# A LoRA-plus-paged-attention kernel: first adapters loaded by a register's number, row numbers on GpSimd, gathers, weight reads and the last outputs in other places

## The chip, the cores and the metric

One core of a Trainium2 chip runs the whole kernel. The metric is the device time of one execution in microseconds; the time before is the median of three runs.

## The reference, cut to what matters

All tensors are float32. There are B = 8 sequences of S = 128 rows and HID = 512 columns, 16 adapters of 512 x 512, 32 query heads and 8 key heads of D = 128, and a cache of 64 pages of 32 positions, of which every sequence uses 16 pages (L = 512 positions).

```python
x = x + einsum("bsi,boi->bso", x, weight[adapter_ids])       # one adapter for each sequence
q, k, v = x @ Wq.T, x @ Wk.T, x @ Wv.T                       # 32, 8 and 8 heads of 128
q, k = rope(rmsnorm(q) * q_norm_w, pos), rope(rmsnorm(k) * k_norm_w, pos)   # pos = seqlen + row
k_all = concat(k_cache[block_table], k)                      # 512 cached positions, then 128 new ones
v_all = concat(v_cache[block_table], v)
scores = q @ k_all.T * SCALE, with cached positions >= seqlen masked
o = softmax(scores) @ v_all                                  # each key head serves 4 query heads
out = x + o @ Wo.T
```

## The kernel before, in words

**Tiling.** The eight key heads are cut into G = 4 groups of two (GK = 2), with the eight query heads that belong to them (GQ = 8). A step is one group of one sequence; there are 32 steps, group by group, eight sequences in each (L216). A step has eight score slots, h = 0 to 7, one for each query head: j = h // 4 is the key head. In a slot (L942 to L1045) TensorE multiplies q by all 640 keys into PSUM (`sc`, L953), VectorE (DVE) adds the mask and takes the minimum of the row (L963; q is scaled negatively, so that is the maximum), ScalarE (ACT) takes the exponential with its sum (L979), VectorE the reciprocal (L1021), and GpSimd (POOL) scales the row (`p`, L1028). One slot later VectorE transposes the 32 x 32 blocks of `p` into `tp` (L808). After four slots `tp` is sent to DRAM (`xp`, L826) and read back with whole blocks exchanged (`pT`, L835), so that the transposition costs TensorE nothing. q (`tq`, `xq`, `qT`) and the cached keys (`tk`, `xk`, `kT`) go the same way; all these DMAs stand in SP's queue, in program order.

**The rest of a step.** Between the scores TensorE gets pieces of a list `main` (L917 to L940), dealt out by cost over the eight slots (L1008 to L1015): for the step that follows, the projections `kv`, `q0` and `q1` (`project`, L649, four matmuls of 128 x 512 each); for the step before, the values `o` of its two key heads (`values`, L770, five matmuls each), and its output `out` (`output`, L786, eight matmuls). From step 6 on ("early") the projections of kv and q0 come ahead of the first values. In group 0 the adapter's product `y` of a later sequence (`lora_y`, L526), its transposed weights `lw` (`turn_lora`) and the transposes of x (`turn_x` before the product is added, `turn_x1` after) come on top; their slots are written out by hand in L224 to L245. What a finished group of matmuls still needs on the other engines is put into a list `pending` and run in the next slot.

**Normalization.** `rotate` (L585) squares q on ScalarE, multiplies by the rotary tables CW and SW on VectorE and adds on GpSimd (L617, L624). `norm_scales` (L626) makes the scale on GpSimd (`ss`, `rs`, L631, L632); ScalarE then applies it (L637). Every engine works in the order in which its instructions were issued, so a scale waits behind whatever stands ahead of it on GpSimd.

**Gathers.** GpSimd issues the indirect DMAs: `kc` (L563) and `vc` (L569), four for each step and each kind, one for 128 cached positions, and the adapters' weights (`gather_lora`, L202). kc has one buffer, vc has two. Their row numbers `key_ix` and `val_ix` are computed at the start (L303). In step i the kc of step i + 2 is issued after slots 2 and 3 (in step 0 after 4 and 5), and the vc of step i + 1 after slots 5 and 6 (L1031 to L1038).

**Weights of later groups.** A piece of weights (128 x 512) is loaded by ScalarE's queue (`load_next`, L270), transposed in 32 x 32 blocks by VectorE and sent to DRAM (`send_weights`, L460), and read back with the blocks exchanged (`receive_weights`, L471), all on ScalarE's queue. The slots of these turns and reads, counted as 8 x step + h, are in L255 to L267; kv, q0 and q1 of the next group are read back in the group's last but one and last step, Wo's pieces in the second step of the new group. Each of the tiles kv, q0, q1, o0 and o1 has one buffer.

**Start and end.** The order of the start is written out in L862 to L911: small tables, the angles of the rotary embedding (`rope_angles`, L366), row numbers, then for sequence 0 the transposed x, kv weights, adapter (`lw`), the product `y`, q0 weights, x again with the product added, and the first projections. Transposes go through PSUM tiles of the pool `ps_mm`, which has four. ScalarE copies most of them out. In the last step the second half of p is transposed by TensorE (`pt`, L818), and behind the loop stand the last values and the last output (L1048 to L1056).

Of the kernel before, what the change touches and what calls it, by code (L numbers as in the profile page):

```python
# [18 lines left out]
P = 128  # L19
# [33 lines left out]
def lora_then_paged_attention(  # L53
# [47 lines left out]
    nc.sync.dma_start(out=ids_i, in_=adapter_ids.partition_broadcast(P))  # L101
# [43 lines left out]

    load_first("kv", 0, 2, nc.sync)
    load_first("kv", 2, 2, nc.scalar)
    bt_i = work.tile([P, 4, S], I32, tag="oT0", name="bt_i")
# [6 lines left out]
    nc.scalar.dma_start(out=wn[:, 0, :], in_=q_norm_w.partition_broadcast(P))  # L155
    nc.scalar.dma_start(out=wn[:, 1, :], in_=k_norm_w.partition_broadcast(P))
# [28 lines left out]
    for m in masks:  # L185
        nc.gpsimd.memset(m[:, :, LC, :], 0.0)


    lora_ix = const.tile([P, B], I32, name="lora_ix")
    nc.vector.scalar_tensor_tensor(  # L190
        out=lora_ix,
        in0=ids_i,
        scalar=float(HID // 4),
        in1=par.to_broadcast([P, B]),
        op0=ALU.mult,
        op1=ALU.add,
    )
    lora_rows = lora_w.rearrange("m (p j) i -> (m p) (j i)", j=4)

    lraw = {}  # L200

    def gather_lora(b, dst=None):  # L202
        if dst is None:
            dst = lora.tile([P, 4, REP, QK], FP, tag="raw", name=f"lraw_{b}")
            dst = dst.rearrange("p a r k -> p (a r k)")[:, 0 : 4 * HID]
        lraw[b] = dst
        nc.gpsimd.indirect_dma_start(
            out=dst,
            out_offset=None,
            in_=lora_rows,  # L210
            in_offset=bass.IndirectOffsetOnAxis(ap=lora_ix[:, b : b + 1], axis=0),
        )
# [11 lines left out]
    for i, (g, b) in enumerate(steps):  # L224
        if i == 0:
            at(i, 1, True, lambda: turn_x1(1))
            at(i, 3, False, lambda: turn_q(0, 1))
            at(i, 7, False, lambda: turn_q(1, 0))
            for n, h in enumerate((5, 6, 6, 7)):
                at(i, h, False, lambda n=n: turn_weights(("o0", 0, n)))  # L230
            for n, h in enumerate((7, 8, 9, 10)):
                at(i, h, False, lambda n=n: turn_weights(("o1", 0, n)))
        if i == last:
            at(i - 1, 6, False, lambda: turn_q(last, 0))
            at(i, 2, True, lambda: turn_q(last, 1))
        at(i, 2, True, lambda i=i: turn_k(i, 1), 1)
        if i < last:
            at(i, 6 if i else 7, False, lambda i=i: turn_k(i + 1, 0), 1)
        if g == 0 and b + 2 < B:
            at(i, 0, True, lambda b=b: turn_x(b + 2))  # L240
            for c in range(KC):
                at(i, c if i else c + 2, False, lambda b=b, c=c: turn_lora(b + 2, c))
            at(i, 8, True, lambda b=b: turn_x1(b + 2))
# [11 lines left out]
    for g in range(1, G):  # L255
        before = 8 * B * (g - 1)
        for k, kind in enumerate(("kv", "q0", "q1")):
            for n in range(4):
                turn_when[before + 9 + 3 * (4 * k + n)] = len(turns_of)
                turns_of.append((kind, g, n))  # L260
                h = (2, 3, 5)[k]
                read_at(before + 8 * (B - 2) + h + n, (kind, g, n))
        for k, kind in enumerate(("o0", "o1")):
            for n in range(4):
                turn_when[before + 46 + 3 * (4 * k + n)] = len(turns_of)
                turns_of.append((kind, g, n))
                read_at(8 * (B * g + 1) + k + n, (kind, g, n))  # L267
# [9 lines left out]


    gather_lora(0, first["lora"])
    load_first("q0", 0, 4, nc.gpsimd)  # L280
    gather_lora(1)

    def more_loads():

        nc.vector.memset(first["q1"][:, 0:1], 0.0)
        load_first("q1", 0, 4, nc.sync)
        load_x(1)
        load_x(2)

        for k in range(2):  # L290
            for n in range(4):
                t = (acc, x1T)[k][B - 4 + n]
                raw[f"o{k}", 0, n] = t if k == 0 else t.rearrange("p c s -> p (c s)")
                nc.sync.dma_start(out=raw[f"o{k}", 0, n], in_=weight_rows(f"o{k}", 0, n))


# [6 lines left out]
    def row_numbers():  # L303
        sel = const.tile([P, 3], FP, name="sel")
        for k in range(3):
            nc.vector.tensor_scalar(sel[:, k : k + 1], inner, 8.0 * (k + 1), None, ALU.is_ge)

        sk = const.tile([P, 1], FP, name="sk")
        nc.vector.scalar_tensor_tensor(
            out=sk, in0=inner, scalar=4.0, in1=quad, op0=ALU.mult, op1=ALU.add  # L310
        )
        for k in range(3):
            nc.vector.scalar_tensor_tensor(
                out=sk, in0=sel[:, k : k + 1], scalar=-32.0, in1=sk, op0=ALU.mult, op1=ALU.add
            )
        nc.vector.tensor_scalar(sk, sk, float(G), None, ALU.mult)
        sv = const.tile([P, 1], FP, name="sv")
        nc.vector.tensor_scalar(sv, inner, float(G), None, ALU.mult)
        temp = work.tile([P, GK, D], FP, tag="k", name="pages").rearrange("p h d -> p (h d)")
        bt_f = temp[:, 0 : 4 * B * LC].rearrange("p (c q) -> p c q", q=4)  # L320
        page = temp[:, 4 * B * LC : 5 * B * LC]
        step = temp[:, 5 * B * LC : 6 * B * LC]
        nc.vector.tensor_copy(bt_f, bt_i)
        nc.vector.tensor_copy(page, bt_f[:, :, 0])
        for k in range(3):
            nc.vector.tensor_tensor(step, bt_f[:, :, k + 1], bt_f[:, :, k], ALU.subtract)
            nc.vector.scalar_tensor_tensor(
                out=page, in0=step, scalar=sel[:, k : k + 1], in1=page, op0=ALU.mult, op1=ALU.add
            )
        nc.vector.scalar_tensor_tensor(  # L330
            out=key_ix[:, 0, :],
            in0=page,
            scalar=float(PSIZE * G),
            in1=sk.to_broadcast([P, B * LC]),
            op0=ALU.mult,
            op1=ALU.add,
        )
        for r in range(4):
            rows = slice(32 * r, 32 * r + 32)
            nc.vector.scalar_tensor_tensor(  # L340
                out=val_ix[rows, 0, :],
                in0=bt_f[rows, :, r],
                scalar=float(PSIZE * G),
                in1=sv[rows, :].to_broadcast([32, B * LC]),
                op0=ALU.mult,
                op1=ALU.add,
            )
        for g in range(1, G):
            nc.vector.tensor_scalar(key_ix[:, g, :], key_ix[:, 0, :], float(g), None, ALU.add)
            nc.vector.tensor_scalar(val_ix[:, g, :], val_ix[:, 0, :], float(g), None, ALU.add)  # L350
# [148 lines left out]
    def group(name, pieces, after):  # L499
# [3 lines left out]
        def piece(k, operands):  # L503
            if k == 0:
                if len(pending) > 1:
                    run(pending)
                y[0] = ps_mm.tile([P, HID], FP, tag="mm", name=name)
# [7 lines left out]
    def add_to_acc(b, store=False):  # L515
        def after(y):
            def add():
                nc.vector.tensor_tensor(acc[b], y, acc[b], ALU.add)
                if store:
                    nc.sync.dma_start(out=out[b], in_=acc[b])  # L520
# [249 lines left out]
    def values(i, j):  # L770
# [8 lines left out]
        def after(o):  # L779
            s.oT[j] = work.tile([P, REP, S], FP, tag=f"oT{j}", name=f"oT_{i}_{j}")  # L780

            pending.append(lambda: nc.scalar.copy(s.oT[j].rearrange("p h s -> p (h s)"), o))  # L782
# [3 lines left out]
    def output(i):  # L786
        g, b = steps[i]
        s = st[i]
        return group(
            f"out_{i}",  # L790
            [
                lambda h=h: (s.oT[h // 4][:, h % 4, :], weights_of(f"o{h // 4}", h % 4))
                for h in range(GQ)
            ],
            add_to_acc(b, g == G - 1),
# [66 lines left out]
    on_act, on_vec = nc.scalar.copy, nc.vector.tensor_copy  # L862
    table_set(AF.Sin)
    rope_angles()
    more_loads()
    row_numbers()
    turn_x(0, on_act)
    for n in range(4):
        turn_weights(("kv", 0, n), on_act)
    rope_cos()  # L870
    rope_table(1)
# [4 lines left out]
    for c in range(KC):  # L876
        turn_lora(0, c, on_act)
    for _, f in lora_y(0):
        f()
    for n in range(4):  # L880
        turn_weights(("q0", 0, n), on_act)
    flush()
    turn_x1(0, on_vec)
    rope_table(0)
# [13 lines left out]
    run(pending)  # L898
    for c in range(LC):
# [9 lines left out]
    make_mask(0)  # L909

# [4 lines left out]
    for i, (g, b) in enumerate(steps):  # L915
# [19 lines left out]
        if early:  # L935
# [3 lines left out]
        if i and i != last - 1:  # L939
            main += output(i - 1)  # L940
        unit = None
        for h in range(8):  # L942
# [88 lines left out]
            if i < last:  # L1031
                k = h - 2 if i else h - 4
                if k in (0, 1) and i + 1 < last:
                    gather_k(i + 2, 2 * k)
                    gather_k(i + 2, 2 * k + 1)
                if h in (5, 6):
                    gather_v(i + 1, 2 * h - 10)
                    gather_v(i + 1, 2 * h - 9)  # L1038
# [10 lines left out]
    pieces = output(last)  # L1049
    for part in (values(last, 0), pieces[0:4], values(last, 1), pieces[4:]):  # L1050
# [52 lines left out]
```

## Time and profile before

| what | value |
|---|---|
| median of 3 runs | 1225.86 us (1223.85 to 1227.68) |
| the profiled execution's own time | 1230.35 us |
| its span | 1228.5 us |
| mean granted clock of TensorE | 0.987 |
| DMA traffic | 328.26 MB, 267 GB/s in the mean |
| scores, L953 | 1024 matmuls (two forms), 321.6 us |
| values, L509 `o` | 640 matmuls, 305.5 us |
| projections of q, L509 `pj_q` | 512 matmuls, 238.7 us |
| output, L509 `out` | 512 matmuls, 235.1 us |
| projections of kv, L509 `pj_kv` | 256 matmuls, 118.1 us |
| GpSimd: gathers of kc and vc | 256, about 1.0 us each |
| GpSimd: scaling of p | 252, 0.80 us each |

The page gives busy times of each engine in one execution. PE is TensorE's matmuls, PEld its weight loads, which run beside them; a float32 matmul appears as two instructions. "Idle before" is the time in which an engine stood still ahead of an instruction, and the releaser is what ended it. The waits list adds up these idle times for each pair of waiting and releasing instruction. The chain lists, in order of time, the work that led to the last instruction. SPq and ACTq are the DMA issues of SP and ScalarE.

### The profile page before, as it was taken

To read this page: it belongs to the slowest core of one execution; us is meant where nothing else is said; L and a number is where in the kernel's file an instruction comes from. 1 tells how busy PE (TensorE), PEld (TensorE's weight loads), DVE (VectorE), ACT (ScalarE), POOL (GpSimd) and SP (SyncE) were. 2 spreads that over 40 slices of the span, in tenths; PEclk is the share of its full clock that TensorE was granted. 3 is DMA by queue.
4 is the path that set the end of the run, shared out by engine and by line. 5 is a ranking of instruction groups with operands and counts; after the bars stand their busy time and mean duration, and the time that the engine had idled before them with its cause. 6 is when DMAs were issued, how large, how long until landed. Compare 5 with 4: busy or idle time off the path is not lost.

```text
span 1228.5 us, 12918 instructions
## 1 busy us (share of the span) xinstructions
PE 1190.2 (97%) x3392; PEld 578.0 (47%) x3392; DVE 733.7 (60%) x1681; ACT 529.8 (43%) x1649; POOL 672.1 (55%) x765
## 2 busy tenths in 40 slices
PE   6979999999899999999999999999999999999988
PEld 4535544554444444444444444444444444444433
DVE  5455566656666666666666666666666655566631
ACT  4445444444444444444444444444444444444432
POOL 5463555454655655566556555666556555666340
PEclk8989999999999999999999999999999999999989
DMA  8256878786988999888998998889997987777741
GB/s 298 86 197 203 302 266 271 258 292 225 335 271 291 295 312 301 276 286 290 310 330 273 308 319 289 286 269 301 301 343 247 301 289 244 260 244 260 237 166 57
DMA packets 187320, 328.26 MB, mean 267 GB/s; under 512 B 13424, under 2 KB 106480, under 8 KB 178160
## 3 DMA queue, kind: packets, MB, share of 16 engines
q1 hardware_dynamic: 123440, 236.22, 57.8%
q10 hardware_dynamic: 50096, 48.22, 12.1%
q0 software_dynamic: 13712, 43.01, 9.9%
q8 instruction: 27, 0.44, 0.1%
q14 instruction: 45, 0.37, 0.1%
HBM read 195.27 MB, written 132.12 MB: 266 GB/s over the span
## 4 chain that ended last, share of the span: by engine, by line
PE 88%; DMA 6%; POOL 2%; ACT 2%; issue 1%; DVE 1%; ACTq 0%; DVEq 0%; POOLq 0%; SPq 0%
PE sc L953 21%; PE o L509 21%; PE pj_q L509 17%; PE out L509 16%; PE pj_kv L509 9%; PE y L509 2%; DMA xp<-tp 2%; DMA w_q<-xw_q 2%; PE lw L431 1%; DMA raw_lora<-in_L_cond_weight_dram,lora_ix 1%; DMA qT<-xq 1%; DMA pT<-xp 1%; PE x L431 1%; PE kt L708 0%; POOL vc L556 0%
## 5 line engine op out<-in xcount | busy, mean ns | idle before, releaser
L963 DVE CUSTOM_DVE_ANT_0 p<-sc,mask 128x640 f32<-128x640 f32 x256 | 210.8, 823 | 404.1 <-PE sc L953 404.0
L979 ACT ACTIVATE p<-p,mn 128x640 f32<-128x640 f32 x256 | 211.6, 827 | 325.1 <-DVE mn L963 319.6
L953 PE MATMUL sc<-kT,qT 128*128 128x512 f32 (+1 forms) x1024 | 321.6, 437 | 9.2 <-DMA qT<-xq 3.7
L1028 POOL TENSOR_SCALAR p<-p,rc 128x640 f32<-128x640 f32 x252 | 201.5, 800 | 214.6 <-DVE rc L1021 211.6
L953 PEld LDWEIGHTS sc<-kT,qT 128*128 128x128 f32 x1024 | 190.8, 191 | 238.2 <-issue 212.4
L509 PE MATMUL o<-pT,vc 128*128 128x512 f32 x512 | 240.1, 599 | 4.2 <-DMA pT<-xp 4.2
L509 PE MATMUL pj_q<-w_q,x1T 128*128 128x512 f32 x512 | 238.7, 596 | 0.4 <-DMA w_q<-xw_q 0.4
L509 PE MATMUL out<-w_o,oT 128*128 128x512 f32 x512 | 235.1, 593 | 0.8 <-ACT oT L782 0.7
L808 DVE STREAM_TRANSPOSE tp<-p 128x640 f32<-128x640 f32 x252 | 210.8, 836 | 13.9 <-POOL p L1028 13.5
L556 POOL DMA_INDIRECT kc<-in_L_cond_k_cache_dram,key_ix x128 | 131.0, 1023 | 39.0 <-issue 31.2
L556 POOL DMA_INDIRECT vc<-in_L_cond_v_cache_dram,val_ix x128 | 129.6, 1013 | 37.8 <-issue 30.5
L637 ACT ACTIVATE q<-q,rs 128x128 f32<-128x128 f32 x256 | 81.9, 391 | 153.5 <-POOL q L624 133.6
L509 PEld LDWEIGHTS out<-w_o,oT 128*128 128x128 f32 x512 | 92.7, 190 | 95.8 <-issue 93.2
L509 PEld LDWEIGHTS o<-pT,vc 128*128 128x128 f32 x512 | 93.1, 193 | 94.8 <-issue 82.8
L509 PEld LDWEIGHTS pj_q<-w_q,x1T 128*128 128x128 f32 x512 | 92.9, 192 | 93.0 <-issue 90.5
L509 PE MATMUL pj_kv<-w_kv,x1T 128*128 128x512 f32 x256 | 118.1, 600 | 0.9 <-ACT x1T L433 0.9
L617 POOL TENSOR_TENSOR k<-sw 128x256 f32<-128x256 f32 x31 | 22.9, 740 | 148.9 <-PE kt L708 136.4
L624 POOL TENSOR_TENSOR q<-q,sw 128x512 f32<-128x512 f32 x61 | 77.0, 1262 | 46.8 <-DVE sw L608 46.8
L592 ACT ACTIVATE sq<-pj_q 128x128 f32<-128x128 f32 x256 | 70.7, 276 | 48.0 <-PE pj_q L509 39.9
L632 POOL TENSOR_TENSOR rs<-ss,mhalf 128x6 f32<-128x6 f32 x64 | 77.2, 1207 | 5.3
L509 PEld LDWEIGHTS pj_kv<-w_kv,x1T 128*128 128x128 f32 x256 | 46.6, 193 | 47.4 <-issue 45.5
L509 PE MATMUL o<-pT,vn 128*128 128x512 f32 x128 | 65.4, 593 | 0.0
(113 smaller groups left out, 868.6 us busy)
## 6 DMA issues: line engine op xcount, KB each, us to landing
xp<-tp SPq DMA_DIRECT2D x63, 1280.0 KB, 5.9
pT<-xp SPq DMA_DIRECT2D x63, 1280.0 KB, 6.8
xk<-tk SPq DMA_DIRECT2D x31, 512.0 KB, 7.6
kT<-xk SPq DMA_DIRECT2D x62, 256.0 KB, 6.4
xq<-tq SPq DMA_DIRECT2D x59, 256.0 KB, 4.9
qT<-xq SPq DMA_DIRECT2D x59, 256.0 KB, 6.0
st_q<-in_L_cond_Wq_dram ACTq DMA_DIRECT2D x24, 256.0 KB, 4.3
xw_q<-tw_q ACTq DMA_DIRECT2D x24, 256.0 KB, 3.5
```

The source lines that it names most:

```text
L431: nc.tensor.transpose(t[:, j, :], blk, ident)
L509: nc.tensor.matmul(y[0], lhsT=lhsT, rhs=rhs, start=(k == 0), stop=(k == len(pieces) - 1))
L556: nc.gpsimd.indirect_dma_start(out=dst[:, c, :], out_offset=None, in_=src, in_offset=bass.IndirectOffsetOnAxis(ap=rows[:, g, at : at + 1], ...
L592: nc.scalar.activation(sq, t[:, h, :], AF.Square, scale=float(D) ** -0.5, accum_out=ss[:, h : h + 1])
L624: nc.gpsimd.tensor_tensor(dst, cw, sw[:, 0:heads, :], ALU.add)
L632: nc.gpsimd.tensor_tensor(rs[:, 0:width], ss[:, 0:width], mhalf[:, 0:width], ALU.pow)
L637: nc.scalar.activation(q, q, AF.Identity, scale=rs[:, h : h + 1])
L808: nc.vector.transpose(u.tp[:, :, r, :], u.p.pop(r).rearrange("q (a k) -> q a k", a=4))
L953: nc.tensor.matmul(sc[:, lo:hi], lhsT=s.qT[j][:, r, :, :].rearrange("d h q -> d (h q)"), rhs=s.kT[j].rearrange("d a c i -> d (a c i)")[:, ...
L963: nc.vector.tensor_tensor_reduce(out=p, in0=sc[:, 0:LA], in1=masks[i % 2].rearrange("p a c i -> p (a c i)"), scale=1.0, scalar=3.0e38, op0 ...
L979: nc.scalar.activation(p, p, AF.Exp, bias=unit.mn[:, one], scale=-1.0, accum_out=unit.sm[:, one])
L1028: nc.gpsimd.tensor_scalar(q, p, unit.rc[:, one], 1.0, ALU.mult, ALU.mult)
```

## The change

It has these parts:

- **First adapters.** The adapters of sequences 0 and 1 are no longer gathered by GpSimd. SP loads the adapter's number into a register and issues a plain DMA with that number in its address (`load_lora`). The one for sequence 0 is the first thing in SP's queue; then come the first half of kv, q0 (before on GpSimd's queue), x 1, adapter 1, q1, x 2 and the eight pieces of Wo of group 0. The function `more_loads`, which held q1 and what follows back until the angles were done, is gone. Adapters 2 to 7 are gathered as before; the numbers for that (`lora_ix`) are made later.
- **Small loads.** The adapters' ids for the gathers come on ScalarE's queue, behind the second half of kv; the two norm weights come on GpSimd's queue.
- **Row numbers.** Their constants are made first on VectorE (`row_parts`); VectorE then converts the page table (`row_numbers`), and the rest of the arithmetic, 14 instructions, is on GpSimd. VectorE adds the group's number (`row_tables`): group 0 in the start, the others after the keys of step 0 are scaled.
- **Order of the start.** For sequence 0 the adapter's transposes come before those of kv, the last two kv pieces after the product y, and the angles' sine and cosine after the first two kv pieces on ScalarE. The rotary tables are both made after `turn_x1(0)`. One of two equal masks is left out.
- **Slots.** In step 0 `turn_x1(2)` is one slot later. kc is gathered after slots 3 and 5 (step 0: 4 and 5), vc after slots 6 and 7 (step 0: all four after 7). Turns of kv, q0 and q1 are 2.5 slots apart instead of 3, those of Wo at slots 39, 42, 45 and 62 to 70. Reads of q0 begin one slot later, of q1 two, of o1 one.
- **End.** In the last step three matmuls of the output of step 30 come ahead of the last values of step 30, whose result is copied at once. The last output is computed and stored in two halves of 256 columns, the second on ScalarE's queue.

```diff
+    def load_lora(b, dst):
+        n = nc.values_load(
+            adapter_ids.unsqueeze(0)[:, b : b + 1],
+            engines=[mybir.EngineType.SP],
...
+        )
+        lraw[b] = dst
+        nc.sync.dma_start(
+            out=dst.rearrange("p (j i) -> p j i", j=4),
+            in_=lora_w[bass.ds(n, 1), :, :].rearrange("m (p j) i -> p (m j) i", j=4),
+        )
...
+    load_lora(0, first["lora"])
     load_first("kv", 0, 2, nc.sync)
     load_first("kv", 2, 2, nc.scalar)
+    load_first("q0", 0, 4, nc.sync)
+    load_x(1)
+    load_lora(1, lora_tile(1))
+    load_first("q1", 0, 4, nc.sync)
+    load_x(2)
...
+    nc.scalar.dma_start(out=ids_i, in_=adapter_ids.partition_broadcast(P))
...
+    nc.gpsimd.dma_start(out=wn[:, 1, :], in_=k_norm_w.partition_broadcast(P))
+    nc.gpsimd.dma_start(out=wn[:, 0, :], in_=q_norm_w.partition_broadcast(P))
...
-            at(i, 8, True, lambda b=b: turn_x1(b + 2))
+            at(i, 8 if i else 9, True, lambda b=b: turn_x1(b + 2))
...
-                turn_when[before + 9 + 3 * (4 * k + n)] = len(turns_of)
+                turn_when[before + 9 + 5 * (4 * k + n) // 2] = len(turns_of)
                 turns_of.append((kind, g, n))
-                h = (2, 3, 5)[k]
-                read_at(before + 8 * (B - 2) + h + n, (kind, g, n))
-        for k, kind in enumerate(("o0", "o1")):
-            for n in range(4):
-                turn_when[before + 46 + 3 * (4 * k + n)] = len(turns_of)
-                turns_of.append((kind, g, n))
-                read_at(8 * (B * g + 1) + k + n, (kind, g, n))
+                read_at(before + 8 * (B - 2) + (2, 4, 7)[k] + n, (kind, g, n))
+        for n, slot in enumerate((39, 42, 45, 62, 64, 66, 68, 70)):
+            key = (f"o{n // 4}", g, n % 4)
+            turn_when[before + slot] = len(turns_of)
+            turns_of.append(key)
+            read_at(8 * (B * g + 1) + n - n // 4 * 2, key)
...
         nc.vector.tensor_copy(bt_f, bt_i)
...
+            nc.gpsimd.tensor_tensor(step, bt_f[:, :, k + 1], bt_f[:, :, k], ALU.subtract)
+            nc.gpsimd.tensor_scalar(step, step, sel[:, k : k + 1], 1.0, ALU.mult, ALU.mult)
+            nc.gpsimd.tensor_tensor(key, key if k else bt_f[:, :, 0], step, ALU.add)
+        nc.gpsimd.tensor_scalar(key, key, float(PSIZE * G), sk, ALU.mult, ALU.add)
...
+    row_parts()
     table_set(AF.Sin)
+    turn_x(0, on_act)
+    for c in range(KC):
+        turn_lora(0, c, on_act)
+    for n in range(2):
+        turn_weights(("kv", 0, n), on_act)
+    row_numbers()
     rope_angles()
-    more_loads()
-    row_numbers()
-    turn_x(0, on_act)
-    for n in range(4):
-        turn_weights(("kv", 0, n), on_act)
-    rope_cos()
-    rope_table(1)
+    row_tables((0,))
...
-        if early:
+        if early and i < last:
             main += values(i - 1, 1)
...
-        if i and i != last - 1:
+        if i == last:
+            pieces = output(i - 1)
+            main += pieces[:3] + values(i - 1, 1, True) + pieces[3:]
+        elif i and i != last - 1:
             main += output(i - 1)
...
-                k = h - 2 if i else h - 4
-                if k in (0, 1) and i + 1 < last:
-                    gather_k(i + 2, 2 * k)
-                    gather_k(i + 2, 2 * k + 1)
-                if h in (5, 6):
-                    gather_v(i + 1, 2 * h - 10)
-                    gather_v(i + 1, 2 * h - 9)
+                if i + 1 < last and h in ((3, 5) if i else (4, 5)):
+                    c = 0 if h < 5 else 2
+                    gather_k(i + 2, c)
+                    gather_k(i + 2, c + 1)
+                for c in {6: (0, 1), 7: (2, 3)}.get(h, ()) if i else (range(LC) if h == 7 else ()):
+                    gather_v(i + 1, c)
...
-    pieces = output(last)
-    for part in (values(last, 0), pieces[0:4], values(last, 1), pieces[4:]):
+    halves = [output(last, half) for half in range(2)]
+    both = halves[0][0:4] + halves[1][0:4]
+    for part in (values(last, 0), both, values(last, 1), halves[0][4:], halves[1][4:]):
```

## The prediction

> **What bounds the kernel now.** I read the page's busy times first, then the waits of PE, then the chain of work round each long PE wait, then the timeline of the engine that the chain blames.
>
> ```profile
> PE 1190.2 (97%) x3392; PEld 578.0 (47%) x3392; DVE 733.7 (60%) x1681; ACT 529.8 (43%) x1649; POOL 672.1 (55%) x765
> ```
>
> TensorE is the bound: 97% of a span of 1228.5 us. The diff adds no matmul work (the last output's matmuls become twice as many of half the width), so it can win only in the 38 us (1228.5 - 1190.2) in which PE is idle, and in time in which PE is slow. The waits of PE (us in total, times, longest) name the idle places:
>
> ```profile
> PE kt L708 <- ACT qT L718: 4.8, 1, 4.8
> PE o L509 <- DMA pT<-xp: 4.2, 1, 4.2
> PE sc L953 <- DMA qT<-xq: 3.7, 1, 3.7
> PE sc L953 <- ACT kT L709: 3.0, 3, 1.4
> PE x L431 <- DVE acc L530: 2.0, 1, 2.0
> ```
>
> All are single events. The first and last lie at the end of step 0 (80 to 91 us), the second in the last step (1183.9 to 1188.1), the third at the change from head group 0 to 1 (332.9 to 336.6), and of the fourth 1.4 at the change to group 2 (615.7). Between them the chain shows steps of 40.7 us (group 0) and 34.6 us (later) with no gap. The start is a chain of its own (start us, us, what):
>
> ```profile
> 0.73 3.55 DMA ids_i<-in_itok_B_dram
> ...
> 4.85 11.11 DMA raw_lora<-in_L_cond_weight_dram,lora_ix
> ...
> 16.10 3.64 PE lw L431 x16
> 19.75 3.61 PE y L509 x8
> ...
> 26.54 3.67 PE pj_kv L509 x8
> ```
>
> The first projection waits for the adapter's weights: ids, a row number on DVE, a gather issued on GpSimd that lands at 15.96.
>
> After an idle stretch PE is also slow. After the 4.24 us of the last step, four o matmuls take 3.78 instead of 1.72 and the next scores 2.13 instead of 1.08: 3.1 us more. After the 3.71: scores 1.67 for 1.08, pj_kv 4.77 for 3.44: 1.9. At the end of step 0: scores 2.52 for 1.08, x transposes 1.94 for 0.9, o 3.66 for 2.58: 3.6.
>
> **What the Trainium skill says.** (1) "TensorE: Matmul & The Clock Gate", What's actually happening: PE falls to half clock after a window of about 3.4 us without activity, and needs such a window of work to rise. The trace agrees (3.71 and 4.24 us of idle were paid for, 1.42 was not: scores 1.35); a stretch of 2.0 us at 61 was paid for too, so little idle is no guarantee. (2) "DMA: Bandwidth & Descriptors", SWDGE vs HWDGE vs iDMA: GpSimd's DMAs have their descriptors written by software, SP's and ACT's by hardware with faster setup. Here the GpSimd gather took 11.1 us, the 0.5 MB of Wv issued on ACT 6.4. (3) "SBUF — State Buffer", SBUF: two separate sides: GpSimd and DVE share a port pair, and one can block the other for an instruction; no row here shows it. (4) Price: a register load from HBM, "Runtime: NRT & Kernel Launch", launch sequence, about 1.3 us; no row here has one.
>
> **The change, part by part.**
>
> *Start.* Removed from the path: ids 3.55, the DVE row number, the gather. Added: two dependent register loads on SP (pointer, value), 1.2 to 2.6 us between both taken as one and each as one; I take 2. The 1 MB DMA is then issued near 2.8, at the head of SP's queue; kv, q0, x1, lora 1, q1, x2 and eight Wo pieces follow it there and are each some 2 us later than nothing ahead would make them, but q0 leaves GpSimd's queue and q1 no longer waits until 11.6. With 0.78 MB (x0, Wv) on ACT and near 380 GB/s (the best microseconds of this start), it lands near 9. PE then: lw 3.6 to 12.7, two kv transposes, y 14.5 to 18, DVE add 1.1 to 19.2. Behind comes ACT: sin, cos and the table load wait for the angles. Those are late now: DVE's cast of the page table (L323) stands ahead of them and waits for its DMA (landed near 9.2 here, expected near 10), then 5 us of angles. ACT's last table is loaded near 19.5, six copies of 0.53 follow, and four PSUM buffers hold x's transposes behind them: x1T near 22.3 instead of 26.4. So **-4.0**. Bounds: -6 (adapter at 8, no wait for angles) to 0. The zero end is GpSimd's 14 small row-number operations: at 0.20 to 0.25 each (128x6 tensor_scalar: 0.20) 3.5 us, hidden beside the angles; at 0.74 each (128x256 add) 10 us, and then DVE's two table adds wait, and behind them in order the cosine, y's add and x1T. The gathers of k and v follow near 16 as before (14.99); their first reader is at 38. The two weight-norm loads go to GpSimd; they are needed near 22 and cost GpSimd two issues of about 1 us ahead of the row numbers, at a time when it waits. Loading lora 1 and q1 in this order costs nothing: readers at 21 and 30, q1 expected near 20. DVE's six later table adds (1 us) lie in the 1.9 us in which it waits for y_1; one mask fewer (0.48) was hidden too.
>
> *Step 0.* GpSimd's four v gathers move from h=5 and 6 to h=7:
>
> ```profile
> 77.81 0.95 POOL L556 DMA_INDIRECT vc<-in_L_cond_v_cache_dram,val_ix  x1 [0.30 <-issue]
> 79.06 0.95 POOL L556 DMA_INDIRECT vc<-in_L_cond_v_cache_dram,val_ix  x1 [0.30 <-issue]
> 80.08 0.24 POOL L631 TENSOR_SCALAR ss<-ss 128x4 f32<-128x4 f32 x1
> ...
> 82.72 0.40 ACT L637 ACTIVATE q<-q,rs 128x128 f32<-128x128 f32 x1 [4.00 <-POOL q L624]
> ```
>
> ss could start two gathers earlier, 2 x 1.25 = 2.5; DVE's sw (done 78.3) does not hold it. ACT's scaling, qT, kT and PE's kt follow in order: -2.5. The gathers now delay p_0 of step 1, whose rc comes at 94.5 here, so 5 us of them fit. x_2's transposes move one slot, so o_0 need not wait for DVE's add: -2.0. Slow clock afterwards: between 0 and all 3.6 saved; I take half, -1.7. Together **-6.2** (-3.5 to -8).
>
> *Group changes* (three). Weight reads move to slots kv 2, q0 4, q1 7 (from 2, 3, 5), and the o turns leave the busy stretch. Before, up to three reads of 0.25 MB and a turn fell in one slot; DMA share was 1.06 and ACT's own issues blocked it for up to 4.75 us:
>
> ```profile
> L474 ACTq DMA_DIRECT2D w_q<-xw_q x24: 366/520/4752, 313.6 to 900.0; - x24
> ...
> DMA to landing us min/median/max: 3.3/8.5/11.3
> ```
>
> I expect the old stalls gone: 3.7 + 1.9 + 1.4 + 0.3 + 0.4 = 7.5. But a new wait comes: the last q1 read is issued at h=2 of the step before the new group, after the exp, 10.9 us into it, and q1's projection starts there after sc_3 and one o: 3 x 4.33 + 1.08 + 0.86 = 14.9. That leaves 4.0 us, and all of PE is queued behind. Reads outside the crowd (339.6, 334.7, 618.6, 896.9) landed in 3.3, 6.0, 5.4, 5.6: mean 5.1; with the queues spread I take 5.2, a stall of 1.2, three times 3.6. Net **-3.9**. Bounds: -7.5 (3.3 us) to +10.9 (landing at the old median, 8.5, stall 4.5 and 1.65 of slow clock each: 18.4). o's later reads leave over 7 us before their reader: nothing, unless they land as late as 9.1 (their maximum).
>
> *End.* Here the cause is two engines away from the wait:
>
> ```profile
> 1165.57 1.11 POOL L556 DMA_INDIRECT vc<-in_L_cond_v_cache_dram,val_ix  x1 [5.24 <-PE o L509]
> ```
>
> GpSimd sat 5.24 us before a gather whose buffer PE was still reading; behind it stood q1's norm, p_6 and p_7, then the transpose, xp (1175.65) and pT, landed at 1188.1. The gathers now stand behind p_6 and p_7's turn comes near 1168 instead of 1173.9, so pT lands near 1182, before PE asks (1183.9). Besides, three matmuls of the next output (2.6) and a score (1.1) now stand ahead of the waiting ones. The copy of oT at once makes ACT wait for o; behind it stand pT copies that PE reads 5 us later: 0. So 4.2 + 3.1 + 0.3 (a wait at 1173.5) are gone, and the split last output saves some 0.3 (half of the 0.69 add): -7.9; I take **-7.5** (-2.6, only the filling, to -8). What is late next: pk's chain, about 4.5 us from score to transpose, with 7 us of work ahead.
>
> Elsewhere gathers only change places on GpSimd (55% busy), with the reader a step or more away: 0, hidden under PE; a wait there costs its excess over that slack.
>
> Sum: -4.0 - 6.2 - 3.9 - 7.5 = -21.6. The profiled execution took 1230.35 (span 1228.5 and 1.9 round it), so 1208.7 of that kind; it lies 4.5 above the median 1225.86, from which the same sum gives **1204.3**.
>
> **Rivals.**
> - *B: q1's weights become the group-change wait.* For: 4.0 us of room against a median of 8.5. Against: the crowd is what made 8.5. At 7 us of landing a stall of 3.0 and 1.65 of slow clock, 14 in three instead of 3.6: 1225.86 - 11.2 = 1214.6.
> - *C: the front yields little.* Row numbers at 0.74 and a clock still slow after step 0: start 0, step 0 -3.5: 1225.86 - 14.9 = 1211.0. Against: 0.20 rows.
> - *D, slower:* the same q1 read, landing at the old maximum 11.3 behind a blocked ACT issue of 4.75: 12.0 of stall and 1.65, 41 in three, 1225.86 - 21.6 + 37.4 = 1241.7. It decides from a landing of 10.7 (three times 6.7 + 1.65 eat 21.6 + 3.6). Against: o's turns no longer share the stretch.
> - *E: the register load does not hasten the adapter* (it lands at 14 or later since all loads now compete): start 0, others as forecast: 1208.3; within the range.
>
> **Numbers.** Forecast 0.48, B 0.20, C 0.15, D 0.05, E 0.10; 0.02 for the rest. Best ends together give 1225.86 - 29.5 = 1196.4; the upper end takes in B and C: 1196 to 1217. A measurement here tells about 0.3% (3.7 us): faster 0.92, same 0.03, slower 0.05.
>
> **What would show it.** lw at 9 to 10 and pj_kv near 22.5; kt's wait near 2.3; no wait for pT in the last step; pj_q's wait for w_q in steps 7, 15, 23 of about 1 us. A wait for w_q over 3 us, or DVE's key_ix waiting for GpSimd past 18, makes it wrong.

## The result and the profile after

| | us |
|---|---|
| before, median of 14 runs on the chip of the comparison | 1227.5 |
| after, median of 14 runs | 1228.9 |
| ratio after to before, 95% interval | 1.0002 (0.9985 to 1.0019) |
| profiled execution before, after (span) | 1230.35 (1228.5), 1228.89 (1227.1) |
| forecast, range | 1204.3, 1196 to 1217 |

No change that can be measured, where 1.7% was forecast. The busy line of the page hardly moves. Busy time includes matmuls at a slow clock: with the same matmuls, run 4 below has 1182.3 for PE.

```profile
PE 1188.1 (97%) x3408; PEld 579.5 (47%) x3408; DVE 729.9 (59%) x1670; ACT 531.0 (43%) x1649; POOL 675.3 (55%) x778
```

These are the longest waits of PE after the start (window 90 us to the end; us in total, times, longest), to be read against those of before:

```profile
PE sc L977 <- DMA qT<-xq: 4.1, 1, 4.1
PE pj_q L508 <- DMA w_q<-xw_q: 4.0, 1, 4.0
PE pj_q L508 <- issue: 3.9, 1, 3.9
```

The waits for pT (4.2), for ACT's kT and for DVE's acc are gone, and kt's is 2.2 instead of 4.8. In their place stand two waits of pj_q, one named for w_q and one for nothing ("issue"). To see what each is worth, take the start of the first scores of some steps from the trace:

| first scores of step | before | after | difference | what lies since the row above |
|---|---|---|---|---|
| 0 | 44.2 | 43.9 | -0.3 | the start |
| 2 | 134.0 | 127.2 | -6.8 | step 0, and step 1 with its slow clock |
| 7 | 336.6 | 330.2 | -6.4 | steps 2 to 6, with the wait for qT in both |
| 8 | 373.0 | 368.8 | -4.2 | first group change (0.6 of wait and 1.4 more of slow clock behind the wait for qT) |
| 15 | 617.2 | 612.1 | -5.1 | Wo's reads +0.9; an old wait (1.4) and its slow clock gone -1.8 |
| 16 | 651.9 | 653.4 | +1.5 | second group change |
| 23 | 894.7 | 896.6 | +1.9 | Wo's reads +0.9; an old wait gone -0.5 |
| 24 | 930.0 | 937.0 | +7.0 | third group change |
| 31 | 1166.0 | 1173.0 | +7.0 | |
| end | 1228.5 | 1227.1 | -1.4 | the last step -8.4 |

Steps 0 and 1 brought 6.5 and the last step 8.4, 14.9 together; steps 2 to 23 gave 13.8 back. The chain at step 15 of the changed kernel (start, us, what) shows how:

```profile
623.30 0.05 ACT p L1003
623.36 8.19 DMA w_q<-xw_q
631.54 0.24 issue
631.78 5.28 PE pj_q L508 x6
```

The last read of q1's weights is issued at 623.36, behind ACT's exp, and lands 8.19 us later. PE had work until 627.8, waited 3.96, and then took 5.28 for six matmul instructions that take 2.58 at full clock. The stretch that holds this (us, PE busy and its instructions, granted clock, DMA share, GB/s) has half the clock:

```profile
629.90:636.80 6.90, 5.02 (x6) 0.51 0.40 144
```

So the place costs 6.7 us over a step's 34.6, not 4.0. At step 23 the same read is issued at 907.88 and lands in 8.2; PE idles 3.88 ahead of 916.23 (the wait without a name), the six take 4.51, and the place costs 5.8. Only at step 7 did the read land in 4.9, with 0.6 of idle. "TensorE: Matmul & The Clock Gate" of the Trainium skill (What's actually happening) has this: an idle window of about 3.4 us halves the clock, until such a window of work. Both waits, 3.96 and 3.88, were paid for again in slow matmuls, with 2.7 and 1.9. Shorter waits were as well (after 3.22 in run 2 the six took 4.50), so staying under 3.4 is no safe bound here.

The other weight reads are hardly what made the late read slow. When it was issued, the one before it was still in flight and landed within 1.5 us (at 624.85 and 909.14). But pT's read (1.25 MB) and the write of the keys, xk (0.5 MB), left within 0.5 us of it at steps 15 and 23, and landed in 6.7 to 8.0 where a landing is on record. At step 7 these two had left 4.2 and 2.0 us ahead of it. That they are what slows it is read from the trace; no run separates it.

The start's chain in the changed kernel:

```profile
3.14 10.08 DMA bt_i<-in_itok_Bx_dram
...
13.24 0.24 DVE pages L334
...
13.90 0.81 POOL pages L337
...
20.58 0.04 DVE val_ix L349
...
20.67 0.43 DVE rope_sw L397
...
21.77 1.28 ACT L360
```

The adapter, issued at 2.67, landed at 12.5 (forecast 9), the page table at 13.2 (forecast 10); the row numbers on GpSimd took from 13.56 to 20.55, and the cosine's DVE operation stood behind them. The first kv projection began at 26.40, before at 26.54.

### The profile page after: what moved, and what is told of

It reads as the page before. It is cut to its first block, busy times and chain, and to the rows that moved or that the text cites. A ratio compares the mean times of both kernels' runs of the same rounds, so it can differ in the third digit from the quotient of the medians.

```text
span 1227.1 us, 12945 instructions
## 1 busy us (share of the span) xinstructions
PE 1188.1 (97%) x3408; PEld 579.5 (47%) x3408; DVE 729.9 (59%) x1670; ACT 531.0 (43%) x1649; POOL 675.3 (55%) x778
## 4 chain that ended last, share of the span: by engine, by line
PE 91%; DMA 3%; POOL 2%; ACT 2%; issue 1%; DVE 1%; ACTq 0%
PE sc L977 22%; PE o L508 21%; PE pj_q L508 18%; PE out L508 17%; PE pj_kv L508 9%; PE y L508 2%; DMA qT<-xq 1%; PE lw L430 1%; DMA bt_i<-in_itok_Bx_dram 1%; DMA w_q<-xw_q 1%; DMA xq<-tq 1%; DMA w_o<-xw_o 1%; PE x L430 1%; PE kt L711 1%; ACT sq L595 0%
## 5 line engine op out<-in xcount | busy, mean ns | idle before, releaser
L508 PE MATMUL pj_q<-w_q,x1T 128*128 128x512 f32 x512 | 242.6, 605 | 8.5 <-DMA w_q<-xw_q 4.0
L508 PE MATMUL o<-pT,vc 128*128 128x512 f32 x512 | 237.4, 594 | 0.0
L508 PE MATMUL out<-w_o,oT 128*128 128x512 f32 (+1 forms) x528 | 235.1, 580 | 2.1 <-ACT oT L786 0.7
L508 PEld LDWEIGHTS out<-w_o,oT 128*128 128x128 f32 x528 | 95.7, 190 | 95.1 <-issue 91.5
```

Source lines behind the costliest of these rows:

```text
L508: nc.tensor.matmul(y[0], lhsT=lhsT, rhs=rhs, start=(k == 0), stop=(k == len(pieces) - 1))
```

## The experiments

The theory after the result: the late last q1 read, with the slow clock behind its wait, eats the gains of step 0 and of the last step. The rival: queues are crowded at a group change wherever a read is put, so that a PE that comes earlier only waits elsewhere. Ratios below are to the kernel before, on the same chip, with 95% intervals. From run 5 on, only the intervals of runs 9 and 12 lie clear of run 4's; what the others gain or lose is read from their traces.

**1. All of the old schedule in the changed kernel.** The loop that fills turn_when and reads_at is put back.

```
-                turn_when[before + 9 + 5 * (4 * k + n) // 2] = len(turns_of)
+                turn_when[before + 9 + 3 * (4 * k + n)] = len(turns_of)
...
-                read_at(before + 8 * (B - 2) + (2, 4, 7)[k] + n, (kind, g, n))
+                read_at(before + 8 * (B - 2) + (2, 3, 5)[k] + n, (kind, g, n))
...
```

> The changed kernel with the whole weight schedule (turns and reads) of the kernel before. Theory: the new schedule's last read of q1's weights, 4 us ahead of its reader, cost 13.8 us at the three group changes and hid the gains of step 0 (6.5) and of the last step (8.4). Without it the three group changes cost what they did before, so about 1227.5 - 15 = 1212 us, with no wait of pj_q for w_q over 1 us. Rival (whatever PE saves is given back at the next tight place, since transfers that take 8 us meet a PE that comes earlier): the stalls come back in other places, 1222 or more.

Measured: 1215.3, ratio 0.9870 (0.9847 to 0.9893). Step 15 takes 34.8, step 23 35.4. The theory holds.

**2. Only the new schedule in the kernel before.** The same loop, the other way.

> The kernel before with only the weight schedule (turns and reads) of the changed one. Theory: the schedule alone loses what the trace showed at steps 7 to 24, 1227.5 + 13 = 1241 us, waits of pj_q for w_q near 4 us at steps 15 and 23. Rival (the late stalls came from the changed order of gathers on GpSimd or from PE being earlier, not from the schedule): within 3 us of the kernel before.

Measured: 1245.4, ratio 1.0115 (1.0090 to 1.0139). The waits of PE after 90 us:

```profile
PE pj_q L508 <- DMA xq<-tq: 4.5, 1, 4.5
...
PE pj_q L508 <- issue: 3.2, 1, 3.2
```

These are the waits at steps 15 and 23 (PE starts again at 640.10 and 923.69, with 5.13 and 4.50 us for the six). The view names xq, the write of the q tiles, for one and nothing for the other; the projection reads neither xq nor tq, and the last q1 reads left at 631.1 and 916.0. A releaser that the consumer does not read is a sign to look for another. Runs 1 and 2 with the two kernels make a square: the schedule costs 1.3% in one corner and 1.15% in the other, so it acts by itself, whatever else was changed.

**3. The old reads, the new turns.**

```
-                read_at(before + 8 * (B - 2) + (2, 4, 7)[k] + n, (kind, g, n))
+                read_at(before + 8 * (B - 2) + (2, 3, 5)[k] + n, (kind, g, n))
...
-            read_at(8 * (B * g + 1) + n - n // 4 * 2, key)
+            read_at(8 * (B * g + 1) + n // 4 + n % 4, key)
```

> The changed kernel, its turns of weights kept, only the reads at the slots of the kernel before (first reads of kv, q0, q1 at slots 2, 3, 5 of the step, Wo's at 0 and 1). The last q1 read then is issued 12.7 us ahead of its reader. Theory: no wait for w_q, 1210 to 1213 us (the spread turns may save a little of the old group-change stalls too). Rival (crowded queues: reads that are packed again land in 8 to 11 us, ACT is blocked in issuing for up to 4.7 us, and exps come late): waits on ACT of 2 to 4 us at the group changes, 1216 to 1222.

Measured: 1213.0, ratio 0.9849 (0.9824 to 0.9874). No wait for w_q. ACT's longest issue of such a read was 1.75, not 4.7, and no wait of PE follows it: here the packed reads do no harm, and the spread turns bring nothing that shows beside run 1 (the intervals overlap).

**4. One number: q1's reads one slot earlier, at 6 instead of 7.**

```
-                read_at(before + 8 * (B - 2) + (2, 4, 7)[k] + n, (kind, g, n))
+                read_at(before + 8 * (B - 2) + (2, 4, 6)[k] + n, (kind, g, n))
```

> The changed kernel with one number changed: q1's reads begin at slot 6 instead of 7. Room for the last read 8.3 us instead of 4.0, against a landing of 8.2 at steps 15 and 23. Theory: the waits of 3.9 and the slow clock behind them go, 1228.9 - 10 to -14 = 1215 to 1219 us. Rival (crowding): the read lands later in its new slot, among q0's reads, and the wait stays at 2 us or more: 1223 or more.

Measured: 1214.1, ratio 0.9858 (0.9832 to 0.9883), against 1.0002 with slot 7. The same place in the chain now reads:

```profile
621.11 3.44 PE o L508 x8
...
625.63 0.86 PE o L508 x2
626.49 1.72 PE pj_q L508 x4
```

The last read left at 617.3, 9.2 us ahead of its reader. Steps 15 and 23 take 34.8 and 34.6. The rival falls: one slot is enough, and no later group change pays for it (step 9, with Wo's reads, takes 35.9 instead of 35.5). What stays is the wait at step 7 (3.7). The next experiments build on this kernel.

**5. The page table earlier.** Its DMA is moved ahead of Wv's half on ACT.

```
+    nc.scalar.dma_start(
+        out=bt_i.rearrange("p c q -> p (c q)"),
+        in_=block_table.rearrange("b n -> (b n)").partition_broadcast(P),
+    )
     load_first("kv", 2, 2, nc.scalar)
```

> The kernel of the q1_early experiment (its first kv projection at 26.9 us, first scores at 44.5), with the page table's load issued ahead of Wv's half on ACT instead of behind it. There it landed 10.1 us after issue and DVE's cast waited for it until 13.8; behind the cast stand angles, row numbers and cosine. Theory (the page table and the row numbers hold the start): it lands at 5 to 8, the cast follows, the cosine's table is loaded some 4 us earlier, and the first kv projection starts at 23 to 24. Rival (the adapter's weights, landed near 13, hold the start): the projection stays within 1 us of 26.9, since lw cannot start before 12.5 and behind it stand 4 us of lw, 3.6 of y and ACT's copies.

Measured: 1213.6, ratio 0.9877 (0.9853 to 0.9900). The table lands in 5.0 us instead of some 10, its cast runs at 7.2 and the last activation table is loaded at 19.3 instead of 22.4; the adapter lands at 11.0. But the kv projection starts at 25.8, only 1.1 earlier: q1's weights are last now. In SP's order they stand behind the load of x 1, which SP issued only when the first adapter had landed (10.98), and behind the second adapter's register loads; they were issued at 14.32 and landed at 24.75.

**6. The cosine ahead of the row tables.**

```
+    rope_cos()
     row_tables((0,))
...
-    rope_cos()
```

> The kernel of the q1_early experiment with the cosine's DVE operation ahead of the two row-table additions, which wait 0.9 and 1.3 us for GpSimd. Theory (the row numbers on GpSimd hold the cosine, and it ACT's copies): the first kv projection 1.8 us earlier than 26.9, the last table load at 20.6 instead of 22.4. Rival (something else is last there, the adapter or y): no earlier by 0.5 us or more.

Measured: 1212.0, ratio 0.9860 (0.9839 to 0.9880); projection at 26.6, 0.3 earlier, table load at 21.8. A miss of the theory: GpSimd does hold the cosine, but freeing it leaves the adapter last (13.4 in this run, with 13.2 us of PE's own work behind it). The page table also landed 0.7 later than in run 4 (14.5 for 13.8), which is part of why the table load came only 0.6 earlier.

**7. The first adapter from a fixed place.** The choice is left out: sequence 0 gets adapter 0, whatever its number.

```
-    load_lora(0, first["lora"])
+    lraw[0] = first["lora"]
+    nc.sync.dma_start(
+        out=lraw[0].rearrange("p (j i) -> p j i", j=4),
+        in_=lora_w[0:1, :, :].rearrange("m (p j) i -> p (m j) i", j=4),
+    )
```

> The kernel of the q1_early experiment, its first adapter's weights loaded from a fixed place (adapter 0 for the first sequence, whatever its number: the choice is left out), so that no register is loaded ahead of it and the transfer is issued near 0.7 instead of 2.65. Theory (the register's two loads cost the 2 us between): it lands 2 us earlier, near 11. Rival 1 (the queue of SP delivers nothing before 7 us whenever it is started): lands at 12.5 or later as now. Rival 2 (the address from a register makes a transfer slow by itself: 4.4 us from issue to the first bytes, against 1 on ACT): lands at 5 to 8, and the first kv projection stands no more than 1 us earlier, since the page table is then last.

Measured: 1215.7, ratio 0.9892 (0.9871 to 0.9913). Issued at 0.75, it landed 5.6 us later, at 6.3: some 6.7 earlier than in run 4, of which the earlier issue explains 1.9. Yet the projection begins at 27.8, later by 1. The chain is the page table's:

```profile
3.53 9.41 DMA bt_i<-in_itok_Bx_dram
...
12.96 0.24 DVE pages L338
...
21.49 1.28 ACT L364
```

The page table landed 0.9 earlier than in run 4 and ACT's table was loaded 0.9 earlier (21.49 for 22.40). What made the projection later is the clock: PE, through with the adapter early, idled 5.12 us ahead of 21.84, and from there to 28 its granted clock was 0.50, so that the 20 transposes behind the wait for ACT took 1.9 us longer than in run 4. Neither transfer alone held the start.

**8. Wk's half ahead of the register loads.**

```
-    load_lora(0, first["lora"])
     load_first("kv", 0, 2, nc.sync)
+    load_lora(0, first["lora"])
```

> The kernel of the q1_early experiment with Wk's half issued on SP ahead of the register loads of the first adapter. Theory (SP's queue stood empty for 4 us of setting up): Wk's half moves from 2 us on, while the registers are loaded, and the adapter, with nothing left ahead of it, lands as early as now or up to 1.5 us earlier (11.5 to 13). Rival (the adapter then shares the engines with what is ahead): lands 1 to 2 us later, at 14 to 15.

Measured: 1216.5, ratio 0.9895 (0.9861 to 0.9928); the adapter landed at 14.3. It has the rival's number by another cause. The chain's first pieces (SPq L150 are the two register loads):

```profile
0.75 0.44 SPq L138
...
1.23 2.37 SPq L150
...
3.62 3.58 SPq L150
...
7.40 6.91 DMA raw_lora<-in_L_cond_weight_dram
```

Behind a transfer of 0.5 MB the two loads take 5.95 us, on an idle queue 0.87 and 0.84.

**9. The v gathers back at h = 5 and 6.**

```
-                for c in {6: (0, 1), 7: (2, 3)}.get(h, ()) if i else (range(LC) if h == 7 else ()):
+                for c in {5: (0, 1), 6: (2, 3)}.get(h, ()):
```

> The kernel of the q1_early experiment with one part of the change undone: GpSimd's v gathers at the slots of the kernel before (h = 5 and 6 of every step). Theory: at the end of step 0 ss waits for two gathers again, kt's wait goes from 2.6 to about 5 (with its slow clock 2.5 to 4 us), and in the last step GpSimd blocks again for some 5 us ahead of q1's norm, p_6 and p_7, so pT lands 5 to 6 us later and PE waits for it what the 3.7 us of matmuls placed ahead don't cover, 0 to 2 us. Together 1214 + 3 to + 6 = 1217 to 1220. Rival (the moved transposes and the output's order do it all): within 1.5 us of 1214, no wait for pT.

Measured: 1221.6, ratio 0.9921 (0.9895 to 0.9947). kt's wait is 4.8 again and step 1 begins 3.7 later than in run 4; steps 3 and 6 lose 1.4 and 1.6, the last step 1.0. GpSimd's wait is back, but PE's for pT is not (0.2), though pT's read left 12 us later than in run 4 (1180.44 against 1168.48, the last step starting 6.6 later):

```profile
POOL vc L559 <- PE o L508: 5.2, 1, 5.2
```

**10. The order of the end back, the gathers new.**

```
-        if early and i < last:
+        if early:
             main += values(i - 1, 1)
...
-        if i == last:
-            pieces = output(i - 1)
-            main += pieces[:3] + values(i - 1, 1, True) + pieces[3:]
-        elif i and i != last - 1:
+        if i and i != last - 1:
             main += output(i - 1)
...
+    pieces = output(last)
+    for part in (values(last, 0), pieces[0:4], values(last, 1), pieces[4:]):
```

> The kernel of the q1_early experiment with the other part of the end undone: values and outputs of the last two steps in the order of the kernel before, the last output in one piece, the v gathers kept at their new slots. Theory (the gathers free pT, the order only fills): no wait for pT over 1 us, since it lands near 5 us earlier than before; the end costs 0.3 to 1 us more: 1214.5 to 1215. Rival (the order does it): the wait for pT of about 4 us and its slow clock come back, 1217 to 1221.

Measured: 1213.6, ratio 0.9860 (0.9834 to 0.9885); last step 54.7 us (run 4: 54.1, run 9: 55.1, before: 62.6). Either part alone removes the wait for pT with its slow clock: gathers that come later bring pT earlier (7.9 off the last step), matmuls ahead bring its reader later (7.5). Their gains do not add: both together bring 8.4.

**11. Three edits at the start together.** Those of runs 5 and 6, and:

```
+    load_first("q1", 0, 4, nc.sync)
     load_x(1)
     load_lora(1, lora_tile(1))
-    load_first("q1", 0, 4, nc.sync)
```

> The kernel of the q1_early experiment with three edits at the start together: the page table's load ahead of Wv's half, the cosine's operation ahead of the row tables, and q1's weights ahead of x1 and of the second adapter's register loads in SP's queue (alone the first gained 1.1 us of the first kv projection, and the second 0.3). Theory (with the table early, q1's weights behind the second register load are last: PE stood 1.8 us in wt_q): first kv projection at 23 to 24 instead of 26.9, the time 1214 - 3 = 1210 to 1212, below both kernels and all runs so far. Rival (it is the adapter's landing at 11 and PE's own work of 12.5 us behind it that holds the start): 25 or later, 1212 to 1214.

Measured: 1211.6, ratio 0.9842 (0.9818 to 0.9866), below both kernels and the lowest so far, though the intervals of runs 1, 3 to 6, 8 and 10 overlap it. The chain, PE without a gap between these lines:

```profile
2.65 8.85 DMA raw_lora<-in_L_cond_weight_dram
...
11.54 3.67 PE lw L430 x16
...
24.62 3.61 PE pj_kv L508 x8
```

The projection begins at 24.5, the first scores at 42.2 instead of 44.5 in run 4: between the two expectations, and what is last now is the rival's: the adapter and PE's own 13 us behind it.

**12. The new order of a step from step 5.**

```
-        early = i >= B - 2
+        early = i >= B - 3
```

> The kernel of the q1_early experiment, in which the order of a step with the projections ahead of the values starts at step 5 instead of step 6. In step 6 the transfer of the next q's turned tiles is issued one slot (4.3 us) later than in any later step, and PE waits 3.7 us for it at the start of step 7, at all placements of the weight reads tried so far. Theory (the switch of order coincides with the crowd of the reads for group 1): the wait at step 7 falls under 1 us and step 6 takes 34.6 us instead of 39.9; 1214 - 4 = 1209 to 1211, or less gained if step 5 takes on part of it. Rival (the slot is late for another reason, the last x1 transposes of group 0 or the reads themselves): the wait stays at 3 us or more.

Measured: 1222.8, ratio 0.9923 (0.9893 to 0.9954). The theory falls: the wait at step 7 stays (3.7), and step 5, which now takes 51.0 us instead of 40.7, has another of 5.6 with its slow clock.

**13. No reads for group 1.** This builds on run 11. The twelve reads of the projections' weights are left out, and group 1 computes with group 0's.

```
-                read_at(before + 8 * (B - 2) + (2, 4, 6)[k] + n, (kind, g, n))
+                if g > 1:
+                    read_at(before + 8 * (B - 2) + (2, 4, 6)[k] + n, (kind, g, n))
```

> The kernel of the experiment with three edits at the start, with the twelve reads of the projections' weights for group 1 left out (group 1 computes with group 0's projection weights; turns and writes stay). Theory (the crowd of reads between 302 and 330 us makes the q tiles' write and read slow, 7 and 10 us): both land in 3 to 5 us, PE does not wait at the start of step 7, step 6 takes 34 us instead of 39. Rival (they are late by slot, and queued behind pT on SP): the wait stays at 2 us or more, step 6 at 37 or more.

Measured in two executions: 1206.7, ratio 0.9810 (0.9768 to 0.9852). PE does not wait, step 6 takes 36.0 us instead of 39.1 and step 7 34.6 instead of 36.4. The stretch from 300 to 330 us, of run 11 and then of this run (PE, PEld, DVE, ACT, POOL busy, clock, DMA share, GB/s):

```profile
300.00:330.00 30.00, 27.10 (x71) 12.56 (x70) 15.26 (x37) 12.24 (x39) 19.22 (x21) 0.96 0.93 297
```

```profile
300.00:330.00 30.00, 30.00 (x82) 14.17 (x82) 16.80 (x41) 13.73 (x46) 20.01 (x22) 1.00 0.73 244
```

The q tiles' way in run 11:

```profile
310.49 7.21 DMA xq<-tq
...
317.72 9.52 DMA qT<-xq
```

Their write took 7.21 and their read 9.52. Without the twelve reads the write left at the same point of the step (22.2 us into it), the read was issued 5.7 us after the write, and PE did not wait for it. So at step 7 it is the crowd of weight reads, and not the slot alone. Steps 14 and 22 have the same reads and no such wait; there as in step 8 the q tiles are written some 17.5 us into the step, in step 6 at 22 (run 4). Why step 6 is later stays open.

## Why the prediction was wrong

The sum of -21.6 became -1.4 in the profiled executions; its terms:

- *Start, -4.0 forecast, -0.3 measured.* Failed, within its bounds (zero was one of them). The register loads were priced rightly: issue at 2.67 for 2.8. Three sizes were not: the adapter landed at 12.5 for 9, because almost nothing moved after its issue (between 3 and 6 us all DMA engines together 14 to 38 GB/s; in run 7, from a fixed place and issued at 0.75, 366 to 416); the page table at 13.2 for 10; the row numbers took 7.0 us for 3.5. "A 128x6 row took 0.20" was no guide for 128x32 on GpSimd: 0.24 to 0.81, the longest while DVE's angles ran, 0.25 for the last of its kind. "SBUF — State Buffer" (SBUF: two separate sides) lets GpSimd and DVE block each other; the rows fit that, no run separates it. The step also took one transfer for the cause where two were nearly equally late. With the page table early (run 5) the adapter and, behind it in SP's order, q1's weights were last; with the adapter early (run 7) it was the page table. Three edits together (run 11) were needed for 2.3.
- *Step 0, -6.2 forecast, -6.5 measured.* Right in mechanism and size: kt waits 2.2, x_2 waits for nobody. Run 9 puts 3.7 of it down to the gathers.
- *Group changes, -3.9 forecast, +13.8 measured.* The step that failed. The mechanism was named ("a new wait comes: the last q1 read") and its room, 4.0 us, was near (4.5 from issue to the end of PE's other work). The landing was mis-sized: 5.2, taken from four reads "outside the crowd", "with the queues spread"; it landed in 8.2 at two of three changes, near the old median of 8.5, which the upper bound of that very step took (+10.9, still below the 13.8). The four were the last two reads of the first change and the last but one of the other two; the last ones of these two (8.5 and 8.2, lines below the list) were not among them. The last read of each change took 3.3, 8.5 and 8.2 before, and 4.9, 8.2 and 8.2 after: spreading the reads did not hasten it. The slow clock, 1.9 to 2.7 behind each wait, stood only in the bounds. And "I expect the old stalls gone" was mostly wrong: of its 7.5, 3.7 and 1.9 were the wait for qT at step 7 and its slow clock, which stayed in every run with reads (run 13: it is the crowd); the 1.4 ahead of step 15 was gone in run 1, with the old schedule, and in run 2, with nothing but the new one, so either part of the change removes it. Wo's later reads, priced at nothing, cost 0.9 each at steps 9 and 17; with the old reads (runs 1 and 3) both steps take 34.6.
- *End, -7.5 forecast, -8.4 measured.* Right, though the text gave the filling 2.6 alone. Run 9 shows 7.5 from the order and the split output alone, since the reader then asks when pT has all but landed, late as it is; run 10 shows 7.9 from the gathers alone.

The last q1 reads of the kernel before at its second and third group change, as its trace has them:

```profile
L474 ACTq DMA_DIRECT2D w_q<-xw_q x1: 367/367/367, 621.3 to 621.3; - x1
DMA to landing us min/median/max: 8.5/8.5/8.5
...
L474 ACTq DMA_DIRECT2D w_q<-xw_q x1: 366/366/366, 900.0 to 900.0; - x1
DMA to landing us min/median/max: 8.2/8.2/8.2
```

Rival B had the mechanism and set the landing at 7, rival D at 11.3; with the measured 8.2 and the slow clock the two waits alone cost 12.5. The mistake in method: the mean of reads at other places of the change was used for the last one, which had landings of its own on record. D was said to decide from a landing of 10.7 because the start's 4.0 and the old stalls' 7.5 were counted as safe. Rival C was right about the start. Both signs that the prediction named for its being wrong came: a wait for w_q over 3 us (3.96), and DVE's key_ix waiting for GpSimd past 18 (until 19.1).

## What to carry to other kernels

A transfer's slot is priced by the room to its reader against landing times. Take those of the same transfer at the same place of the step, not the mean of those that came through quickly, and if the room is less, move it one slot (here one number was worth 1.4%). Waits of 3.7 to 4.2 us on TensorE cost another 1.9 to 3.1 in slow matmuls behind them. When two waits end together, removing one brings nothing: look at what is next before pricing a start, and treat two edits against one wait as one gain.

## What the hardware showed that was not expected

- Loading a register from HBM on SP took 0.84 to 0.87 us on an idle queue ("Runtime: NRT & Kernel Launch", launch sequence, gives about 1.3 for a few words), but 2.37 and 3.58 with a 0.5 MB transfer issued ahead of them on the same queue (run 8). What follows such a load in SP's order waits with it: in run 8 the adapter was issued at 7.40, after the two.
- A 1 MB adapter took 5.6 us from a fixed address (run 7), and 6.9 to 10.8 from a register's in the changed kernel and runs 5, 6, 8 and 11. "DMA: Bandwidth & Descriptors" (Specifications) has first bytes after 0.6 us on this path; with the fixed address all engines moved 98 GB/s between 1 and 2 us and 401 between 3 and 4, with the register's (changed kernel, issue at 2.67) 15, 14 and 38 between 3 and 6. The runs do not tell apart how much of that is the address and how much the earlier issue, ahead of the small broadcasts.
- A small page table broadcast to 128 partitions landed in 5.0 and 5.3 us when issued ahead of a 0.5 MB load (runs 5 and 13), in 8.7 to 11.4 behind it (the changed kernel and runs 4 and 6 to 8).
